# Two layers on one core: attention's query and key projection by seven products, sums shared with the FFN

## The chip, the core and the metric

The kernel runs on one core of a Trainium2 chip, in float32 apart from a few small bf16 operands. Its engines work side by side, each through a queue of its own: TensorE (PE, matmuls), VectorE (DVE), ScalarE (ACT), GpSimd (POOL), and SyncE (SP), which here only starts DMAs. The metric is the device time of one launch in microseconds (us), the median over several runs.

## The reference

Two blocks, each `x = x + mixer(norm(x)) + ffn(norm(x))`, on x of shape (2, 1024, 512): two sequences of 1024 rows.

```python
xn = _layernorm(x, axis=-1)                       # layer 0: a small scan and an FFN
x = x + _L0_attn_ref(xn, ...) + _L0_ffn_ref(xn, ...)
xn = _layernorm(x, axis=-1)                       # layer 1
x = x + _L1_attn_ref(xn, ...) + _L1_ffn_ref(xn, ...)

def _L1_attn_ref(x, W_qkv, b_qkv, W_out, b_out):  # 16 heads of 32
    qkv = x @ W_qkv.T + b_qkv
    q, k, v = jnp.split(qkv, 3, axis=-1)
    scores = jnp.einsum('bqhe,bkhe->bhqk', q, k) * scale
    scores = jnp.where(causal[None, None], scores, -jnp.inf)
    out = jnp.einsum('bhqk,bkhe->bqhe', softmax(scores), v)
    return out.reshape(b, l, d) @ W_out.T + b_out

def _L1_ffn_ref(x, w_gate, w_up, w_down):
    h = silu(x @ w_gate) * (x @ w_up)
    return _sparsify_2to4(h) @ w_down
```

Attention and FFN of layer 1 read the same normalized x, and their outputs are added to the same residual. The change touches the two products that give q and k.

## The kernel before

**Stages.** Layer 0 comes first. Then comes layer 1's attention, with the last rows of layer 0's result normalized and transposed in its opening. Layer 1's FFN comes last. The normalized input of layer 1 is held transposed in four tiles `xt1[0..3]`, each 128 partitions x 4 x 512: the four are chunks of 128 of the 512 input features, the 512 are rows of x. `xt1[0]` and `xt1[1]` belong to the first sequence, `xt1[2]` and `xt1[3]` to the second.

**Seven products.** A product of two matrices cut into 2 x 2 blocks takes eight block products. Strassen's scheme in Winograd's form takes seven, with sums of blocks formed beforehand (t1 to t4 on the side of x, s1 to s4 on the side of the weights) and with the seven results added into the four blocks of the output. Layer 1's FFN is already computed this way: `combine_x` (L148) forms the sums of x on DVE (L156, L157, L160, L161; t1, t2 and t4 in tiles of their own, t3 over the first half of the second x), `combine_w` (L165) those of the weights on POOL, and `gate_up` (L186) issues the seven products (L179). The projection of q and k is computed with all eight.

**Attention.** The work is cut into eight units u: a sequence times a group of four heads (`units`, L1020; four groups, `HG`). Between two units lies what is called a boundary below. For each unit and for each of its tiles of 128 queries, `maxima` (L1079) computes the scores once only for their row maxima: the matmuls "m" (L1088, 4 heads of 32 rows each, the two pairs of heads in two PSUM pairs), the causal mask on the diagonal block (DVE, L1095) and the reduction (DVE, L1096). `larger` (L1106) joins the maxima of two column halves. `shift_part` and `shift_rows` (L1116 to L1130) turn the maxima into three bf16 rows. `weights` (L1136) computes the scores again, transposed (the matmuls "s", L1145), adds the shift (L1151), applies exp (ACT, L1162) into `pt` (or `acc` for the first key tile), and cuts the diagonal block to its triangle (POOL, L1171). `gather` (L1180) multiplies with the values (the matmuls "o", L1191) and adds `pt` into `acc` on POOL (L1198). `total` and `divide` sum `acc` over the partitions, take the reciprocal on DVE and multiply `att` by it on POOL (L1222).

**The order of work.** There are 96 slots n, 12 for each unit, after 13 slots of prologue (n from -13 to -1; the loop L1365). In a slot PE does: s of slot n, o of slot n-1, m of slot n+13 (so the maxima run a good unit ahead), and then one "part": two matmuls of 128x512 of the other products of this layer, so q and k (`project`, "pq"), the values (`values`, "pv"), or the output projection (`project_out`, "po"). `piece` (L1024) cuts each of those into two parts, which fill one PSUM bank over four steps of k; the result is taken from the bank after the second part, for q and k by ACT with the bias (L1052). The parts wait in the list `rest` with a first and a last slot each; `one_part` (L1332) takes the one with the earliest last slot, and `late` (L1352) takes more than one in a slot where the last slots ask for it. Other steps are fixed to a slot with `put`, and follow its part. `in_program_order` (L48) binds PE, DVE, ACT and POOL from the mark L1364 on to the order in which this Python code issues instructions; SP's DMAs follow their own. Each of these engines works through its queue in that order, and an instruction that waits holds up all behind it.

**PSUM.** Three pairs of banks (`ps_wide`) rotate among m (two at a time), s (two), and the small transposes; each must be read empty before it is used again. Of the two single banks, bank 0 holds o and bank 1 serves the parts; while there is no o, in the prologue and at the end, parts alternate between the two (`alone`).

**Before and after attention.** Unit 0's q and k are computed in one run of 16 matmuls before the prologue (L1360); the weights of a head group (`wqk`) are loaded by SP. After the last slot the FFN's first input sums are asked for (L1389) and the rest of the output projection follows. The FFN's units are (`pb`, `g`, `half`) (L1405): `pb` is the sequence, `g` a quarter of the hidden width. Its second sequence's sums are asked for by a second `combine_x` inside the FFN.

## Time and profile before

| | us |
|---|---|
| median of 3 runs (1817.91 to 1819.95) | 1819.89 |
| the profiled execution | 1816.24 |
| span of its trace | 1814.5 |
| end of layer 0, first matmul of unit 0's q and k | 665.97 |
| first m (unit 0) | 681.51 |
| first s (unit 0) | 733.52 |
| first product of layer 1's FFN | 1222.77 |

The granted TensorE clock was 0.999. The rows shown below are of four kinds. In the page's first part each engine has its busy time and its number of instructions. In a table of windows each row is a stretch of the span, with its length and with the busy time of PE, PEld (weight load), DVE, ACT and POOL, then the granted clock, the DMA share and their rate. In a timeline each row is a run of like instructions: start, length, engine, line of the kernel, operation, output and inputs by the program's names, shape, and count; in square brackets stands a wait that ended just before and what ended it. A 128x512 float32 matmul has two records. Times of a row are microseconds from the start of the span; lines such as L1088 are those of the kernel above.

### The profile page before, as it was taken

The page shows a single profiled execution, that of the slowest core. Times are in us where ns is not written, and L with a number is a line of the kernel's source. Part 1 is how long each engine was busy: PE and PEld are TensorE (multiplying, and loading weights), DVE is VectorE, ACT ScalarE, POOL GpSimd, SP SyncE. Part 2 cuts the span into 40 slices and gives each one's busy share as a digit, 9 for nine tenths or more (in the row PEclk, how much of TensorE's full clock was granted, in tenths as well). Part 3 has the DMA queues.
Part 4 walks back from the last instruction along what each step waited for, and adds up shares of the span by engine and source line. Part 5 has one row for each costly group of instructions (what it writes and reads, how often), then busy time and mean ns, then how long its engine had stood idle before and what let it go on. Part 6 is the DMA issues. An engine that isn't in the chain of part 4 may idle for free.

```text
span 1814.5 us, 18967 instructions
## 1 busy us (share of the span) xinstructions
PE 1784.9 (98%) x7386; PEld 915.2 (50%) x7386; DVE 1140.8 (63%) x1483; ACT 476.5 (26%) x681; POOL 806.5 (44%) x697
## 2 busy tenths in 40 slices
PE   9999999999999999999999999999999999999999
PEld 5456566555555564333333333334465555555545
DVE  4875544556544448566677666762868778768675
ACT  3322222122221102334333443422212211212220
POOL 5144554355642222467668756613243344243400
PEclk9999999999999999999999999999999999999999
DMA  6120111111101000000001000011010102201101
GB/s 233 47 81 24 47 35 35 28 43 35 35 23 35 12 29 24 1 12 13 13 1 36 12 13 1 25 47 44 26 58 27 55 24 73 89 25 47 47 1 47
DMA packets 29609, 68.12 MB, mean 38 GB/s; under 512 B 3408, under 2 KB 11856, under 8 KB 27984
## 3 DMA queue, kind: packets, MB, share of 16 engines
q1 hardware_dynamic: 28800, 66.61, 11.3%
q8 instruction: 59, 0.97, 0.2%
q10 hardware_dynamic: 720, 0.30, 0.1%
q14 instruction: 30, 0.25, 0.0%
HBM read 62.70 MB, written 4.19 MB: 37 GB/s over the span
## 4 chain that ended last, share of the span: by engine, by line
PE 92%; DVE 5%; ACT 1%; issue 1%; POOL 0%; POOLq 0%; DVEq 0%; ACTq 0%
PE p_a L179 21%; PE p_c L179 20%; PE d L305 19%; PE pq L1036 6%; PE m L1088 5%; PE s L1145 4%; PE o L1191 3%; PE pv L1036 3%; PE po L1036 3%; PE dr L1526 2%; ACT acc L1162 1%; PE s L1151 1%; PE w L1210 1%; PE pp L603 1%; PE pw L439 1%
## 5 line engine op out<-in xcount | busy, mean ns | idle before, releaser
L323 POOL TENSOR_TENSOR x<-x,de 128x512 f32<-128x512 f32 x87 | 126.5, 1469 | 302.1 <-DVE x L318 168.0
L1198 POOL TENSOR_TENSOR acc<-acc,pt 128x1024 f32<-128x1024 f32 (+3 forms) x138 | 233.8, 1717 | 0.0
L1096 DVE TENSOR_REDUCE tops<-m 128x2 f32<-128x1024 f32 (+2 forms) x192 | 180.9, 956 | 58.8 <-PE m L1088 54.3
L318 DVE TENSOR_TENSOR x<-x,d 128x512 f32<-128x512 f32 x145 | 99.3, 685 | 145.5 <-PE d L305 145.3
L1162 ACT ACTIVATE pt<-s 128x1024 f32<-128x1024 f32 (+3 forms) x160 | 115.2, 766 | 177.4 <-PE s L1151 162.2
L305 PE MATMUL d<-td,h 128*128 128x256 f32 x592 | 141.4, 383 | 4.9 <-DVE h L280 4.9
L305 PEld LDWEIGHTS d<-td,h 128*128 128x128 f32 x592 | 113.2, 192 | 48.0 <-issue 29.2
L1036 PE MATMUL pq<-xt,wqk 128*128 128x512 f32 x256 | 124.2, 614 | 0.0
L179 PE MATMUL p_c<-xt,s_c 128*128 128x512 f32 x256 | 115.2, 593 | 3.4 <-DVE e_c L232 3.4
L179 PE MATMUL p_a<-xt,s_a 128*128 128x512 f32 x256 | 116.8, 599 | 0.9 <-DVE e_a L232 0.9
L179 PE MATMUL p_a<-xt,w 128*128 128x512 f32 x256 | 115.4, 593 | 0.7 <-ACT xt L136 0.7
L179 PE MATMUL p_c<-xt,gu 128*128 128x512 f32 x256 | 115.7, 592 | 0.0
L179 PE MATMUL p_a<-t_a,s_a 128*128 128x512 f32 x256 | 115.3, 594 | 0.0
L179 PE MATMUL p_c<-t_c,s_c 128*128 128x512 f32 x256 | 114.6, 592 | 0.0
L1095 DVE TENSOR_TENSOR m<-m,mask 128x256 f32<-128x256 f32 x128 | 54.7, 427 | 84.6 <-PE m L1088 82.5
L1088 PE MATMUL m<-qk,qk 32*128 32x512 f32 (+3 forms) x768 | 102.8, 533 | 3.9 <-ACT acc L1162 3.0
L1145 PE MATMUL s<-qk,qk 32*128 32x512 f32 (+3 forms) x768 | 93.8, 533 | 0.2 <-DVE tops L1096 0.2
L172 POOL TENSOR_TENSOR s_c<-gu,s_c 128x512 f32<-128x512 f32 x16 | 20.4, 1274 | 136.6 <-PE p_c L179 136.6
L179 PEld LDWEIGHTS p_a<-xt,s_a 128*128 128x128 f32 x256 | 47.5, 191 | 59.0 <-issue 58.4
L1088 PEld LDWEIGHTS m<-qk,qk 32*128 32x128 f32 x768 | 39.8, 183 | 72.7 <-issue 24.8
L179 PEld LDWEIGHTS p_c<-xt,s_c 128*128 128x128 f32 x256 | 48.5, 190 | 55.5 <-issue 54.3
L1036 PEld LDWEIGHTS pq<-xt,wqk 128*128 128x128 f32 x256 | 44.3, 189 | 62.5 <-issue 59.5
(250 smaller groups left out, 3049.7 us busy)
## 6 DMA issues: line engine op xcount, KB each, us to landing
w<-in_W SPq DMA_DIRECT2D x32, 512.0 KB, 3.6
gu<-in_gu SPq DMA_DIRECT2D x32, 512.0 KB, 3.6
wd<-in_down SPq DMA_DIRECT2D x8, 1024.0 KB, 4.8
x<-in_x SPq DMA_DIRECT2D x16, 256.0 KB, 4.6
w2h<-in_W2q SPq DMA_DIRECT2D x4, 1024.0 KB, 11.4
xr<-in_x SPq DMA_DIRECT2D x16, 256.0 KB, 2.7
wqk<-in_WqkvT SPq DMA_DIRECT2D x16, 256.0 KB, 3.2
out_x<-x SPq DMA_DIRECT2D x15, 256.0 KB, 2.0
```

The lines of the kernel that those rows point to most:

```text
L179: nc.tensor.matmul(pair[:, m, :], a[:, m, k, :], x[:, k, :], start=start and k == 0, stop=stop and k == 1, skip_group_check=True,)
L305: nc.tensor.matmul(out_[:, j, :], lhs[:, q, j * P : (j + 1) * P], rhs[:, q], start=m in (0, 1, 3, 4) and j == q == 0, stop=j == q == 1, sk ...
L318: nc.vector.tensor_add(r, r, out_)
L323: nc.gpsimd.tensor_add(r, r, u2[half])
L1036: nc.tensor.matmul(got[0], lhs(k), rhs(k), start=(k == 0), stop=(k == KC - 1))
L1088: nc.tensor.matmul(pair[h // 2][:, h % 2, :e], q[rows, qt * P : (qt + 1) * P], k[rows, c * 512 : c * 512 + e], start=True, stop=True,)
L1095: nc.vector.tensor_add(d, d, mask.unsqueeze(1).to_broadcast([P, 2, P]))
L1096: nc.vector.tensor_reduce(out=tops[u][:, c, qt, 2 * p : 2 * p + 2], in_=pair[p][:, :, :e], axis=mybir.AxisListType.X, op=ALU.max,)
L1145: nc.tensor.matmul(pair[h // 2][:, h % 2, s:], k[rows, kt * P : (kt + 1) * P], q[rows, cols], start=True, stop=False,)
L1162: nc.scalar.activation(pt[:, :, s:], pair[p][:, :, s:], AF.Exp, scale=1.0 / math.sqrt(HD))
L1191: nc.tensor.matmul(po[rows, s:], v[:, rows], pts[h // 2][:, h % 2, s:], start=(kt == 0), stop=last, tile_position=(0, h * HD),)
L1198: eng.tensor_add(acc[:, :, s:], acc[:, :, s:], pt[:, :, s:])
```

## The change

The projection of a unit's q and k becomes one chain of seven products. The weights of q and k of a head group are seen as blocks: w11, w12 (q, first and second half of the input features) and w21, w22 (k). The other side is x and y, the two 512-row halves of the unit's sequence, each in its two halves of features. So output blocks are q of x's rows, q of y's rows, and the same for k.

- `project(u)` yields seven parts of two matmuls (n from 0 to 6) in place of eight. Part 0 fills a bank of its own (chain "b"), parts 1 to 4 run on in one bank (chain "a"), whose contents are read after each of them, and parts 5 and 6 share a third (chain "c"). Results go to q and k by ACT (`first`, with the bias) or are added to them by DVE (`more`). In units 1 to 7 ACT takes the bank after parts 0, 2, 3 and 4, and DVE after 1, 5 and 6; since part 2 goes on adding into the bank that part 1 left, it waits for that DVE addition. Unit 0 takes the parts in the order 1, 0, 2, 5, 3, 6, 4, with bank 0 for chain "a" and bank 1 for "b" and "c"; there DVE takes them after 0, 3 and 6.
- The sums of weights go to POOL: three when a unit's first part is issued (`weight_sums`), and a fourth after part 0. Each is 128x256. One is formed in place in w21, the last in w12.
- The sums of x (`input_sums`): for the first sequence five DVE operations in the run before the prologue, ahead of unit 0's products; for the second five POOL operations, put after the parts of slots 24, 25, 28 and 29. t1, t2 and t4 stay in the tiles that `combine_x` uses. t3 is kept in two tiles of the pool of `att`, since the values need y as it is.
- `own_place`, on POOL in slot 52, forms the FFN's t3 over the first half of y of the second sequence, once the values have been taken from it.
- The FFN takes the second sequence first (`for pb in (1, 0)`), because the tiles t1, t2 and t4 hold its sums then. The `combine_x` at the end of attention goes, and the one within the FFN now forms the first sequence's.
- In `rest` a unit has one entry with seven parts instead of four with two. Its last slot is as before. Its first slot is as before, but for the first unit of the second sequence (u = 4) three later. All other parts, fixed steps and loads are asked for in the slots that they had.

```diff
@@ -145,11 +145,15 @@
-    def combine_x(pool, x, y, name):
-        tt = [
+    def three_sums(pool, name):
+        return [
             pool.tile([P, 2, TT], F32, tag=f"t{n}", name=f"t{n}_{name}") for n in (1, 2, 4)
         ]
+    def combine_x(pool, x, y, name):
+        tt = three_sums(pool, name)
         tt.insert(2, y[:, :2, :])
         def first():
@@ -940,6 +944,7 @@
     first_gu = {}
     sums = ctx.enter_context(tc.tile_pool(name="sums", bufs=1))
     with tc.tile_pool(name="b", bufs=1, reuse_waits="tile") as b:
@@ -1021,17 +1026,21 @@
         alone = 0
+        def next_bank(name):
+            nonlocal alone
+            if alone is not None:
+                alone += 1
+            return ps_bank(name, 1 if alone is None else alone % 2)
         def piece(name, lhs, rhs, done):
             got = []
             def part(n):
                 if n == 0:
-                    nonlocal alone
-                    if alone is not None:
-                        alone += 1
-                    got.append(ps_bank(name, 1 if alone is None else alone % 2))
+                    got.append(next_bank(name))
                 for k in (2 * n, 2 * n + 1):
                     nc.tensor.matmul(
                         got[0], lhs(k), rhs(k), start=(k == 0), stop=(k == KC - 1)
@@ -1041,23 +1050,89 @@
             return [(part, 0), (part, 1)]
-        def project(u, m, n):
+        tts = {}
+        def input_sums(bb):
+            x, y = xt1[2 * bb], xt1[2 * bb + 1]
+            t1, t2, t4 = three_sums(sums, f"b{bb}")
+            t3 = [b.tile([P, TT], F32, tag="att", name=f"t3{k}_{bb}", bufs=12) for k in range(2)]
+            tts[bb] = [t1, t2, t3, t4]
+            e = nc.gpsimd if bb else nc.vector
+            yield e.tensor_sub(t1, y[:, :2, :], x[:, :2, :])
+            yield e.tensor_sub(t2, y[:, 2:, :], t1)
+            yield [e.tensor_sub(t3[k], y[:, 2 + k, :], y[:, k, :]) for k in range(2)]
+            yield e.tensor_sub(t4, x[:, 2:, :], t2)
+        def own_place():
+            y = xt1[3]
+            nc.gpsimd.tensor_sub(y[:, :2, :], y[:, 2:, :], y[:, :2, :])
+            tts[1][2] = y[:, :2, :]
+        def project(u):
             bb, hg = units[u]
-            def done(pq):
-                if (u, m) not in qk:
-                    qk[u, m] = b.tile([P, S], F32, tag=f"qk{m}", name=f"qk{m}_{u}", bufs=3)
+            got = {}
+            order = (1, 0, 2, 5, 3, 6, 4) if u == 0 else range(7)
+            def place(m, n):
+                return qk[u, m][:, n * TT : (n + 1) * TT]
+            def first(m, n, bank):
                 nc.scalar.activation(
-                    qk[u, m][:, n * TT : (n + 1) * TT], pq, AF.Identity,
-                    bias=bqk[:, m * HG + hg : m * HG + hg + 1],
-                )
-            return piece(
-                f"pq_{u}_{m}_{n}", lambda k: wqk[hg][:, k, m, :],
-                lambda k: xt1[2 * bb + n][:, k, :], done,
-            )
+                    place(m, n), bank, AF.Identity, bias=bqk[:, m * HG + hg : m * HG + hg + 1]
+                )
+            def more(m, n, bank):
+                nc.vector.tensor_add(place(m, n), place(m, n), bank)
+            def weight_sums(w11, w21, w22):
+                got[2], got[3] = (
+                    sums.tile([P, 2, P], F32, tag=f"sq{n}", name=f"sq{n}_{u}") for n in (2, 3)
+                )
+                nc.gpsimd.tensor_sub(got[3], w11, w21)
+                nc.gpsimd.tensor_add(w21, w21, w22)
+                nc.gpsimd.tensor_sub(got[2], w21, w11)
+            def part(n):
+                x, y = xt1[2 * bb], xt1[2 * bb + 1]
+                t1, t2, t3, t4 = tts[bb]
+                w11, w12, w21, w22 = (
+                    wqk[hg][:, 2 * e : 2 * e + 2, m, :] for m in range(2) for e in range(2)
+                )
+                if n == order[0]:
+                    if (u, 0) not in qk:
+                        for m in range(2):
+                            qk[u, m] = b.tile([P, S], F32, tag=f"qk{m}", name=f"qk{m}_{u}", bufs=3)
+                    weight_sums(w11, w21, w22)
+                chain = "bbaaaacc"[n + 1]
+                lhs = (w12, w11, got[2], got[3], w22, w21, w12)[n]
+                rhs = (x[:, 2:, :], x[:, :2, :], t2, t3, t4, t1, y[:, 2:, :])[n]
+                start, stop = n in (0, 1, 5), n in (0, 4, 6)
+                if start:
+                    got[chain] = (ps_bank(f"pq_{u}_{chain}", int(chain != "a")) if u == 0 else
+                                  next_bank(f"pq_{u}_{chain}"))
+                for k in range(2):
+                    nc.tensor.matmul(
+                        got[chain], lhs[:, k, :], rhs[k] if type(rhs) is list else rhs[:, k, :],
+                        start=start and k == 0, stop=stop and k == 1, skip_group_check=True,
+                    )
+                do, *at = (
+                    (more, 0, 0), (more, 0, 0), (first, 0, 1), (more, 1, 1), (first, 1, 0),
+                    (more, 1, 1), (more, 0, 1),
+                )[n]
+                if n == order[0] or n == 3 and not got.get("c") or n == 5 and u == 0:
+                    do = first
+                do(*at, got[chain])
+                if n == 0:
+                    nc.gpsimd.tensor_sub(w12, w12, got[2])
+            return [(part, n) for n in order]
         def values(bb, n, j):
@@ -1261,6 +1336,13 @@
             after.setdefault(n, []).append(what)
+        second_sums = []
+        def next_sums():
+            if not second_sums:
+                second_sums.append(input_sums(1))
+            next(second_sums[0])
         sums_at = []
         for u in range(len(units)):
@@ -1274,9 +1356,10 @@
                     put_mid(n + 2 + m, shift_part, u, half, m)
                 put_after(n + 5, shift_rows, u, half)
             if u:
-                lo = per * (u - 2) - 1 if u > 1 else -ahead
-                for x in range(4):
-                    rest.append((lo, per * u - ahead - 1, project(u, x // 2, x % 2)))
+                lo = max(per * (u - 2) - 1, -ahead)
+                if u == HG:
+                    lo += 3
+                rest.append((lo, per * u - ahead - 1, u))
             if u > 1:
                 put(max(per * (u - 2) - 4, -ahead), load_qk, units[u][1])
             for j in range(2):
@@ -1292,6 +1375,10 @@
                     put(len(second) + 1, total, u, j)
         for what in sums_at:
             put_after(*what)
+        rest = [(lo, hi, project(u)) for lo, hi, u in rest]
+        for n in (0, 1, 4, 5):
+            put(per * 2 + n, next_sums)
+        put(per * 4 + 4, own_place)
         for x in range(4):
             rest.append((-ahead, x, values(0, 0, x)))
             rest.append((-ahead, 7 + x, values(0, 1, x)))
@@ -1357,11 +1444,12 @@
                 for last in {x[1] for x in rest}
             )
-        for x in range(4):
-            for f, *args in project(0, x // 2, x % 2):
-                f(*args)
         behind = None
         start = mark()
+        for _ in input_sums(0):
+            pass
+        for f, n in project(0):
+            f(n)
         for n in range(-ahead, len(second)):
             if n == 0:
                 alone = None
@@ -1386,9 +1474,7 @@
         gather(*behind)
         alone = 0
         n = len(second)
-        first_tt, *make = combine_x(sums, xt1[0], xt1[1], "c0")
-        for m, f in enumerate(make):
-            put(n + 5 + m, f)
+        first_tt = tts[1]
         while rest or open_parts or fixed:
             one_part(n)
             what_is_fixed(n)
@@ -1402,7 +1488,7 @@
     start2 = mark()
     with tc.tile_pool(name="c", bufs=1, reuse_waits="tile") as c_:
-        units = [(pb, g, half) for pb in range(2) for g in range(G) for half in range(2)]
+        units = [(pb, g, half) for pb in (1, 0) for g in range(G) for half in range(2)]
         groups = len(units) // 2
         gu_w = dict(first_gu)
@@ -1613,7 +1699,7 @@
                 if at == 5 and n % 2 == 0 and n:
                     load_down(n // 2)
                 if at == 5 and n == len(units) // 2 - 1:
-                    next_tt, first, second = combine_x(sums, xt1[2], xt1[3], "c1")
+                    next_tt, first, second = combine_x(sums, xt1[0], xt1[1], "c1")
                     first()
             gate_up(
```

## The prediction

> **What bounds the kernel now.** First the page's busy times, then the window table, because a mean over five different stages says little about the one that is edited.
>
> ```profile
> PE 1784.9 (98%) x7386; PEld 915.2 (50%) x7386; DVE 1140.8 (63%) x1483; ACT 476.5 (26%) x681; POOL 806.5 (44%) x697
> ```
>
> ```profile
> 666.00:734.00 68.00, 67.88 (x261) 28.95 (x263) 47.92 (x85) 15.70 (x24) 13.20 (x14) 1.00 0.06 16
> 734.00:1158.00 424.00, 416.39 (x2818) 145.83 (x2812) 276.29 (x366) 163.08 (x259) 289.93 (x285) 1.00 0.04 11
> ```
>
> The columns are PE, PEld, DVE, ACT, POOL busy. Attention runs from 666 to 1223. PE is "busy" 98% there, which would make every matmul removed worth its full length. Here the Trainium skill speaks against the change (Perfetto Trace Analysis, Identifying the Most-Contended Engine): matmul busy time is a bad measure, because pipelined matmuls look other than they are. I therefore measure from start to start. A 128x512 fp32 matmul is two records of 429 ns (eight records in 3.43 us in the chain), so 0.858 us. By busy share, 16 fewer matmuls save 13.7 us. By starts, it depends on what a slot costs when its "part" (two 128x512 matmuls, 1.91 us with the change of shape) is not there. One slot of before has none:
>
> ```profile
> 1128.35 1.39 PE L1088 MATMUL m<-qk,qk 32*128 32x512 f32 x8
> ...
> 1130.81 0.70 PE L1145 MATMUL s<-qk,qk 32*128 32x512 f32 x2 [0.16 <-DVE tops L1096]
> ...
> 1133.08 0.76 PE L1088 MATMUL m<-qk,qk 32*128 32x256 f32 x8
> ```
>
> ```profile
> 882.19 1.38 PE L1088 MATMUL m<-qk,qk 32*128 32x512 f32 x8
> 883.50 1.98 PE L1036 MATMUL pq<-xt,wqk 128*128 128x512 f32 x4
> ...
> 887.70 0.94 PE L1088 MATMUL m<-qk,qk 32*128 32x256 f32 x8
> ```
>
> It takes 4.73 us against 5.51 for the same slot with a part. Leaving 1.91 us out saves 0.78: the second half of s waits for the maxima (L1096) to free its PSUM pair, which the part used to cover. Each removed part is therefore costed by its own place. The third view is a boundary between two head groups, PE and POOL, where m of the next group, the last s of the old one and POOL's backlog meet:
>
> ```profile
> 908.92 1.17 PE L1088 MATMUL m<-qk,qk 32*128 32x512 f32 x8
> ...
> 913.59 0.50 PE L1088 MATMUL m<-qk,qk 32*128 32x128 f32 x8
> ...
> 917.30 0.42 PE L1191 MATMUL o<-pt,v 128*32 128x128 f32 x8
> ...
> 922.56 1.07 PE L1191 MATMUL o<-acc,v 128*32 128x512 f32 x8
> ```
>
> ```profile
> 916.36 0.78 POOL L1171 TENSOR_SCALAR_AFFINE_SELECT pt<-pt 128x256 f32<-128x256 f32 x2
> 917.10 2.50 POOL L1198 TENSOR_TENSOR acc<-acc,pt 128x512 f32<-128x512 f32 x2
> 919.54 0.78 POOL L1171 TENSOR_SCALAR_AFFINE_SELECT acc<-acc 128x256 f32<-128x256 f32 x2
> ```
>
> POOL runs without a gap here. Its select of pt ends at 917.14 and o starts 0.16 later: POOL sets this o. Its select of acc ends at 920.32, and the o that reads it starts at 922.56: 2.24 us of slack (1.74 at 797.96/799.70, 2.25 at 1043.64/1045.89).
>
> **The change, part by part** (order of instructions read from the built program; sizes from rows of before).
>
> *Removed:* 8 units x 2 matmuls x 0.858 = 13.7 us of PE, as eight parts. In the new order they are missing at: unit 0's opening run (one); the double part just before the first s (one); an m512 with mask before the 128-wide s (three, at the boundaries of units 0/1, 2/3, 4/5); the m512 before the 256-wide s (two, at 2/3 and 4/5); m128 before s512 in unit 6 (one).
>
> *Unit 0.* Gain 1.72. Products 1 and 0 need no sums and run 665.97 to 669.40. Product 2 needs t2. The old FFN sums of the same tiles give its time:
>
> ```profile
> 666.98 1.22 DVE L156 TENSOR_TENSOR t_c<-xt,xt 128x1024 f32<-128x1024 f32 x1
> 668.23 1.22 DVE L157 TENSOR_TENSOR t_c<-xt,t_c 128x1024 f32<-128x1024 f32 x1
> ```
>
> so t2 is there at 669.45: 0.1 us lost. Product 5 takes the bank that product 0 left, and DVE reads that bank only behind t1, t2, two t3 (0.69 each, as other 128x512 adds) and t4: 669.45 + 1.4 + 1.2 + 0.69 = 672.75, where PE could start at 671.2. Lost 1.6; net 0.0. POOL's three weight sums (0.70 each) follow memsets that end at 664.08, so they should be over at 666.3, before t1 starts. If they start only after the last product of layer 0 (666.2), they meet t1 and t2. The Trainium skill (SBUF — State Buffer, Who interferes with whom) says that a DVE instruction with two SBUF inputs and a GpSimd one that reads SBUF exclude each other. The trace agrees: L1106, 128x16, took 0.17 us with POOL idle and 4.62 at 915.73, ending as POOL stopped. Without the rule the net is 0.0, with it and a late start 1.3 lost. I take 0.0, the memset row being the nearer one, and keep 1.3 for the range.
>
> *Unit 1* (prologue, DVE 47.92 of 68.00 us busy, and 14.03 of 15 between 695 and 710). Gain 1.72. Product 2 follows product 1 directly into the same bank, with DVE's add (0.69, like x<-x,po) between: 0.2 drain + 0.69 + 0.1 = 1.0 lost. The waits for ACT around products 3 and 4 cost about 0.2. Two further adds on the full DVE delay the copies and reductions behind them; followed instruction by instruction, a transpose waits for its pair at 701.1 instead of 699.1, about 0.7 more. Net 0.2 lost (from 1.0 gained, if DVE catches up, to 1.5 lost).
>
> *Steady units.* Parts lie a slot (about 5 us) apart, so three DVE adds of 0.69 and four ACT copies a unit are hidden: the add ends 4.3 to 5.2 us after its m, the next part starts later than 5.6. Without that distance each costs the 1.0 of unit 1. ACT keeps four copies.
>
> *The empty slots.* Masked m512 to the next m128 takes 4.67 us at every boundary (908.92 to 913.59): two mask adds and two 1.22 us reductions, which end just before, with PE's own work some 3.9. Leaving the part out gains nothing there (three times 0.0). The two m512 before a 256-wide s gain 4.54 to 3.83, 0.7 each, but PE then waits for POOL's select of pt (917.14), so nothing is left. The m128 slot of unit 6: s could start at 1126.07, and without the part when ACT frees its pair at 1124.7: gain 1.35. POOL was idle before that unit's second half, so it stays.
>
> *Weight sums on POOL.* Four 128x256 operations a unit; L1198 at 128x256 is 0.70 from start to start, so 2.8 us. For units 2, 4 and 6 they fall where POOL idles and hide. For 3, 5 and 7 they stand in POOL's queue just ahead of the select of acc, in the backlog. Behind them wait that select and then o. With the 0.17 from select to o seen above, o comes at 797.96 + 2.85 + 0.17 = 801.0 (was 799.70), 923.3 (922.56) and 1046.7 (1045.89): lost 1.3, 0.8, 0.8. The fourth also waits for product 0, long over.
>
> *Second sequence's sums on POOL* (t1, t2, t4 2.35 each by L1198 128x1024, t3 two of 1.27). t1 to t3 fit into idle time. t4 stands behind the multiplication of att:
>
> ```profile
> 886.65 1.27 POOL L1222 TENSOR_TENSOR att<-att,inv 128x512 f32<-128x512 f32 x1 [2.89 <-DVE inv L1220]
> ```
>
> so it ends at 890.25, and product 4 of unit 4 is due at 888.57: 1.8 lost. The acc adds behind it start 2.35 later; the idle 2.46 before 899.64 covers that. own_place (2.35) falls into a like idle stretch and is hidden; without it, product 3 of unit 6 would wait up to 2 us.
>
> *FFN.* Same instructions in the same order on other tiles; one DVE subtraction (1.16, L160) goes, off the path. The loads and SP's queue keep their order. 0.0.
>
> *Sum:* 0.0 - 0.2 - (1.3 + 0.8 + 0.8) - 1.8 + 1.35 = 3.55 us longer. The profiled span is 1814.5 (execution 1816.24); it becomes 1818.0. The median of the runs shown, 1819.89, lies 3.65 over its own profiled execution; on it the sum gives 1823.4.
>
> **Rivals.**
> *PE-bound after all, faster.* POOL's queue gives way at the boundaries, because it is served sooner than I read it. Then units 0 and 1 keep 1.7 each, the two 256-wide slots 0.7 each and unit 6 1.35: 6.2 shorter, 1813.7. For it: POOL has 134 us idle between 734 and 1158. Against it: the 0.16 at 917.30. It decides if the three selects of acc end less than 1.7 to 2.2 us later than now.
> *DVE locked out by POOL, slower.* L1106 already took 4.6 us at three boundaries, until POOL paused. If POOL's run is 2.8 longer without a pause, the next reductions and the second half of s come 2.5 to 3 later in three places instead of 0.8 to 1.3, and unit 0 meets its 1.3: about 6 more, 1829.5. Against it: each weight sum waits for the one before, which should leave a pause.
> *Nothing moves.* t4 and the prologue are absorbed by slack that I have not seen: 0 to 2 longer, 1821.
>
> **How the numbers follow.** Forecast 0.50 (alone 1821 to 1826.5), lock-out 0.25, faster 0.17, nothing 0.08. A measurement of this kernel can tell about 0.2%, 3.6 us, and the forecast lies on that line: 0.27 of its 0.50 above. Slower 0.27 + 0.25 = 0.52; same 0.23 + 0.08 = 0.31; faster 0.17. The range takes the forecast, nothing and nearly all of lock-out: 1815 to 1831.
>
> **What would show it.** pq at 7/8 of its matmuls; PE waiting on DVE twice before the first m of unit 1; o of acc 0.8 to 1.3 late with POOL's new sums before it; about 1.8 us of PE waiting on POOL for t4; FFN span unchanged. I am wrong if o of acc doesn't wait on POOL, or if stage times outside attention move by over 1 us.

## The result, and the profile after

The changed kernel takes 1826.61 us (median of 5 runs, 1824.40 to 1828.52), the kernel before 1819.10 (5 runs, 1816.78 to 1819.95) beside it: ratio 1.0044, 95% interval 1.0029 to 1.0058. It is slower by 7.5 us, and the interval lies wholly above 1. The forecast was 3.55 slower, 1823.4, with a range of 1815 to 1831. The profiled execution of the changed kernel is 1825.55, its span 1823.8, which is 9.3 over the span before.

The page's first part and two rows of its window table, in the same columns as before:

```profile
PE 1780.7 (98%) x7354; PEld 913.7 (50%) x7354; DVE 1147.9 (63%) x1508; ACT 476.8 (26%) x681; POOL 841.3 (46%) x735
```

```profile
666.00:734.00 68.00, 63.82 (x245) 27.30 (x243) 51.26 (x86) 15.70 (x24) 21.20 (x22) 1.00 0.08 25
734.00:1158.00 424.00, 406.25 (x2757) 143.11 (x2756) 275.14 (x384) 162.09 (x256) 309.88 (x308) 0.99 0.04 11
```

PE has 32 records less (7386 to 7354; 16 matmuls are gone), POOL 35 us more. The clock column of the second row reads 0.99 where it read 1.00. That hundredth is three stretches of 3.41 us at half clock (3 x 0.5 x 3.41 / 424 = 0.012), and much of what follows is about them.

To find the places, I compared the start of every o (one for each slot) in the two traces, counted each from its span's start, and noted where the difference grows:

| stretch | forecast | measured |
|---|---|---|
| layer 0, up to unit 0's first product (665.97, 667.62) | 0 | +1.65 |
| unit 0, to the first m | 0.0 (1.3 if POOL collides with DVE) | +1.21 |
| unit 1 and prologue, to the first o (739.55, 743.14) | +0.2 | +0.73 |
| boundary of units 0/1 | +1.3 | +1.58 |
| boundary 1/2 | 0 | +0.50 |
| t4, slot 30 | +1.8 | +1.73 |
| boundary 2/3 | +0.8 | +1.02 |
| boundary 3/4 | 0 | -0.56 |
| boundary 4/5 | +0.8 | +0.90 |
| slots 61 to 72 | 0 | -0.07 |
| unit 6, slot 76 | -1.35 | -1.07 |
| FFN | 0 | +1.71 |
| sum | +3.55 | +9.33 |

Boundary 2/3 of the changed kernel, PE and POOL (the stretch that was shown of before):

```profile
915.77 1.14 PE L1163 MATMUL m<-qk,qk 32*128 32x512 f32 x8
...
918.84 0.38 PE L1220 MATMUL s<-qk,qk 32*128 32x128 f32 x2 [1.63 <-DVE tops L1171]
...
919.98 0.98 PE L1266 MATMUL o<-pt,v 128*32 128x256 f32 x8 [0.59 <-POOL pt L1246]
920.89 0.50 PE L1163 MATMUL m<-qk,qk 32*128 32x128 f32 x8
921.32 3.68 PE L1121 MATMUL pq_b<-xt,wqk 128*128 128x512 f32 x4
...
930.96 1.06 PE L1266 MATMUL o<-acc,v 128*32 128x512 f32 x8
```

```profile
924.49 2.50 POOL L1273 TENSOR_TENSOR acc<-acc,pt 128x512 f32<-128x512 f32 x2
926.94 0.74 POOL L1097 TENSOR_TENSOR sq<-wqk 128x256 f32<-128x256 f32 x1
...
930.04 0.77 POOL L1246 TENSOR_SCALAR_AFFINE_SELECT acc<-acc 128x256 f32<-128x256 f32 x2
```

From m512 to m128 the slot takes 5.12 us here (4.67 before; the 0.59 of waiting for POOL's select of pt is in it) and 4.67 at the boundary 0/1. So the empty slot gives nothing, as forecast. But the product behind it, the same four records as ever, takes 3.68 us instead of 1.98. The weight sums are where they were expected, and the select of acc ends at 930.81; o of acc starts at 930.96 and shows no wait for it.

The window table again, for the stretches around the three masked empty slots; the column to read is the clock, third from the right (1.00 or 0.50):

```profile
791.76:795.17 3.41, 1.86 (x24) 0.98 (x24) 2.86 (x4) 0.38 (x1) 3.41 (x5) 1.00 0.00 0
795.17:798.58 3.41, 3.41 (x12) 1.17 (x4) 2.15 (x5) 0.38 (x1) 3.41 (x5) 0.50 0.00 0
918.05:921.47 3.42, 2.04 (x25) 1.10 (x26) 2.25 (x4) 0.38 (x1) 3.42 (x5) 1.00 0.00 0
921.47:924.88 3.41, 3.41 (x4) 0.92 (x4) 3.02 (x5) 0.38 (x1) 3.41 (x5) 0.50 0.00 0
1040.93:1044.35 3.42, 1.20 (x17) 0.64 (x16) 3.08 (x4) 0.38 (x1) 3.42 (x5) 1.00 0.01 2
1044.35:1047.76 3.41, 3.41 (x17) 1.60 (x12) 1.81 (x5) 0.38 (x1) 3.41 (x3) 0.50 0.02 5
```

Each time PE is busy for 1.2 to 2.0 of 3.41 us, and the next 3.41 us run at half clock. The distances between these stretches are whole multiples of that length: 921.47 - 795.17 = 126.30 = 37 x 3.413, 1044.35 - 921.47 = 122.88 = 36 x 3.413. The Trainium skill (TensorE: Matmul & The Clock Gate, Part 1: The HAM clock gate) describes this: a monitor looks at PE's activity in windows of 3413 ns that run free of the kernel, and halves the clock after an idle one. The length and the spacing agree with the trace. "Idle" does not: windows with 35% to 60% of PE busy were enough here.

Two rows of the table of stretches (layer 0 and the FFN) are not the change's. Layer 0 of this execution has 6.83 us at half clock from 23.76, the one before had 3.41 from 151.71; the programs don't differ there. In the FFN both kernels have the same stall, before and after:

```profile
1295.81 3.67 PE L179 MATMUL p_c<-xt,s_c 128*128 128x512 f32 x8 [2.48 <-DVE e_c L232]
```

```profile
1303.44 5.37 PE L183 MATMUL p_c<-xt,s_c 128*128 128x512 f32 x8 [2.49 <-DVE e_c L236]
```

A stall of 2.48 us was followed by full clock, one of 2.49 by 3.41 us at half (1303.76). Where the windows fall differs from execution to execution, and with it one such event, 1.7 us. Without these two rows the change costs 9.33 - 1.65 - 1.71 = 5.97 us in this trace.

A half-clock window of 3.41 us takes 0.5 x 3.41 / 1815 = 0.00094 off the mean granted clock. The runs before lie mostly at 0.997 and 0.998, the five runs after at 0.993 to 0.995: some 2 to 5 such windows more, each worth up to 1.7 us. An estimate of their share: of later runs of the kernel before, the six at 0.994 and 0.995 took 1821.4 to 1822.4, and the changed kernel took 1824.4 to 1828.5 at the same two clocks. So of the 7.5 us some 3 go with the clock, and some 4 do not.

### The profile page after: what moved, and what is told of

Same layout as the page of the kernel before. It is cut to its first block, busy times and chain, and to the rows that moved or that the text cites. A ratio compares the mean times of both kernels' runs of the same rounds, so it can differ in the third digit from the quotient of the medians.

```text
span 1823.8 us, 18993 instructions
## 1 busy us (share of the span) xinstructions
PE 1780.7 (98%) x7354; PEld 913.7 (50%) x7354; DVE 1147.9 (63%) x1508; ACT 476.8 (26%) x681; POOL 841.3 (46%) x735
## 4 chain that ended last, share of the span: by engine, by line
PE 89%; DVE 6%; POOL 2%; ACT 2%; issue 1%; DVEq 0%; ACTq 0%; POOLq 0%
PE p_a L183 21%; PE p_c L183 20%; PE d L309 19%; PE m L1163 4%; PE s L1220 4%; PE pv L1045 3%; PE o L1266 3%; PE po L1045 3%; PE pq_a L1121 3%; PE dr L1612 2%; PE pq_c L1121 1%; POOL acc L1273 1%; DVE tops L1171 1%; ACT acc L1237 1%; PE pp L607 1%
## 5 line engine op out<-in xcount | busy, mean ns | idle before, releaser
L1220 PEld LDWEIGHTS s<-qk,qk 32*128 32x128 f32 x768 | 34.3, 183 | 81.8 <-issue 69.8
L183 PEld LDWEIGHTS p_c<-xt,gu 128*128 128x128 f32 x256 | 48.6, 190 | 51.0 <-issue 49.5
L183 PEld LDWEIGHTS p_a<-t_a,s_a 128*128 128x128 f32 x256 | 48.4, 194 | 50.4 <-issue 49.8
```

The source lines that it names most:

```text
L183: nc.tensor.matmul(pair[:, m, :], a[:, m, k, :], x[:, k, :], start=start and k == 0, stop=stop and k == 1, skip_group_check=True,)
L1220: nc.tensor.matmul(pair[h // 2][:, h % 2, s:], k[rows, kt * P : (kt + 1) * P], q[rows, cols], start=True, stop=False,)
```

## The experiments

Two theories for the boundaries. **POOL** is the forecast's: the weight sums delay the select of acc, and o with it. **Clock**: the empty slot leaves a window with little matmul work, and the half clock behind it costs 1.6. A third has both, running beside each other, so that taking one away shows nothing. Times of the kernel before in these comparisons are medians of 24 to 42 runs, 1817.2 to 1817.8, so 1.3 to 1.9 lower than the 1819.10 that stood beside the changed kernel. The changed kernel was not timed again; where a run is compared with it, the distance of each to its own run of before is the fairer measure (7.5 us for the changed kernel). Readings by boundary come from one profiled execution of each kernel.

### Filling the slots, moving the sums, and both

Filled:

```diff
             if n >= 0 or n % 2:
-                one_part(n)
+                if not one_part(n) and n in (10, 34, 58):
+                    spare = ps_bank(f"spare_{n}", 1)
+                    for k in range(2):
+                        nc.tensor.matmul(
+                            spare, xt1[0][:, k, :P], xt1[1][:, k, :], start=k == 0, stop=k == 1
+                        )
```

> The changed kernel, with two 128x512 matmuls whose result nobody reads put into the three slots that the change left empty at the boundaries 0/1, 2/3 and 4/5 (slots 10, 34, 58). Base: the changed kernel, 1826.6 us. In its trace PE idles 1.63 to 1.72 us in these slots, the granted clock is 0.5 for the next 3.41 us, and the first q/k product takes 3.59 us instead of 1.98; o of acc starts 0.15 to 0.23 us after POOL's select of acc ends. Theory two limits at once (the halved clock costs 1.6 at each boundary, and POOL's queue, longer by the weight sums, ends at the same time): no halved clock at the boundaries, but o of acc then waits for POOL; 0 to 0.8 shorter, about 1826.2. Clock alone: 3 x 1.6 = 4.8 shorter, 1821.8. POOL alone (the prediction's step): no change, 1826.6.

Sums later (the four sums in one function, the two tiles taken where they were):

```diff
...
-                    weight_sums(w11, w21, w22)
+                    new_sums()
+                    if u in (3, 5, 7):
+                        put(per * (u - 2), all_sums, w11, w12, w21, w22)
+                    else:
+                        three(w11, w21, w22)
...
-                if n == 0:
+                if n == 0 and u not in (3, 5, 7):
```

> The changed kernel, with the four weight sums of units 3, 5 and 7 put into POOL's queue one slot later, behind the select of acc. Base 1826.6 us. Two limits at once: PE still runs at half clock there, so o of acc starts as late as before; within 0.5, 1826.6. Clock alone: the same, 1826.6. POOL alone: o of acc comes 1.3, 0.8 and 0.8 earlier, 2.9 shorter, 1823.7.

Both edits together:

> Both edits: the three empty slots filled with matmuls that nobody reads, and the weight sums of units 3, 5 and 7 one slot later. Base 1826.6 us. Two limits at once: each boundary gets its 1.6 back only now, 4.8 shorter, 1821.8 (o of acc again starts 1.7 us or more after the select, as before the change). Clock alone: 1821.8 too, but the first of the three runs had it already. POOL alone: 2.9 shorter, 1823.7, as the second run.

Medians: filled 1827.47 (ratio to before 1.0044, 1.0027 to 1.0061), later 1827.19 (1.0053, 1.0038 to 1.0068), both 1826.27 (1.0040, 1.0018 to 1.0062). They lie 9.9, 9.6 and 8.7 over before. The first two are near what the theory of two limits says, but the medians alone decide nothing: the third missed its 1821.8 by far, and half clock at other places, told below, is in all three. So the traces have to say more. What the boundaries cost against before, from the starts of o:

| boundary | changed | filled | later | both |
|---|---|---|---|---|
| 0/1 (slots 11 to 13) | +1.58 | +1.37 | +1.63 | +0.30 |
| 2/3 (slots 35 to 37) | +1.02 | +0.89 | -0.19 | -0.19 |
| 4/5 (slots 59 to 61) | +0.90 | +0.89 | +1.02 | +0.26 |

With the slots filled no window at the boundaries is at half clock, and o of acc now waits for POOL at each of them (1.06, 1.17 and 1.18 us), which no trace had shown so far. At the first:

```profile
801.66 0.72 POOL L1133 TENSOR_TENSOR wqk<-wqk,sq 128x256 f32<-128x256 f32 x1
802.34 0.77 POOL L1246 TENSOR_SCALAR_AFFINE_SELECT acc<-acc 128x256 f32<-128x256 f32 x2
```

```profile
802.80 1.41 PE L1266 MATMUL o<-acc,v 128*32 128x512 f32 x8 [1.06 <-POOL acc L1246]
```

With the sums moved the half clock stays at 0/1 and 4/5, and the time with it; at 2/3 no half clock came in that execution, and the loss is gone. With both edits each boundary gets most or all of its time back. So both limits are real, they run beside each other, and each alone costs about what the other does.

What ate the gain of "both" is the clock at other places. Its profiled execution has half clock for 13.65 us from 1131.77 and for 3.41 from 739.24; slots 76 to 78 come out 4.7 us later than in before, where the changed kernel gained 1.07. The run with filled slots has the same 13.65 us there (from 1131.57, 4.7 later), the run with later sums 6.83 (from 1131.70, 1.8 later); so it is in part chance that their medians come so near to the changed kernel's. Slots 76 and 77 are two empty slots in a row: the changed kernel left the first, the second was empty already. The clock stays down there for four windows although PE is busy throughout by the trace; that the stretch, at half clock, holds too little work in a window to get the clock back is a likely reason, not a shown one. The same slots cost nothing in the profiled execution of the changed kernel. The five runs of "both" lie between 1819.56 (clock 0.999) and 1831.89 (0.991). At like clock the gain is there: "both" took 1819.56 at 0.999 and 1823.30 at 0.997, so about 1821.4 between them, where the one filled run at 0.998 took 1823.91. The columns of the table differ by 2.8 in sum. These are single runs.

### Fewer matmuls in the kernel before

This run asks the question directly: the kernel before, and only work taken away.

```diff
+                half = name in ("pv_0_1_3", "pv_1_0_3", "pq_6_1_1")
-                for k in (2 * n, 2 * n + 1):
+                for k in () if half and n else (2 * n, 2 * n + 1):
...
-                        got[0], lhs(k), rhs(k), start=(k == 0), stop=(k == KC - 1)
+                        got[0], lhs(k), rhs(k), start=(k == 0), stop=(k == (1 if half else KC - 1))
```

> The kernel before, with six 128x512 matmuls left out and nothing else changed: the second halves of one value product each in slots 10 and 34 and of one key product in slot 58 (two steps of k of four, so these three 128x512 results are computed over half of the features only). What follows them on DVE and ACT stays. Base: the kernel before, 1817.2 us. Clock theory: without these parts PE idles 1.6 to 1.7 us at the three boundaries, the next 3.41 us run at half clock, and each boundary comes out 1.6 later; less 0.5 at 2/3 and 4/5, where the lock-out of the join of maxima is then covered: 3.5 to 4.0 longer, 1821. Work theory (PE is the bound, less work is less time): 6 x 0.43 to 6 x 0.86 = 2.6 to 5.2 shorter, 1812 to 1814.6. Neither (empty slots hidden behind DVE, clock unchanged): 1817.2.

1822.08 us (22 runs) against 1817.77 (30): ratio 1.0021, 1.0014 to 1.0028. Six matmuls fewer make the kernel 4 us slower. The mean clock accounts for it: its median over the runs is 0.994 against 0.997, and at equal clock the two kernels take the same (at 0.994, 1822.0 to 1822.5 with six fewer and 1822.1 to 1822.2 before; at 0.996, 1818.9 to 1820.2 and 1819.4 to 1820.8). The three boundaries of its profiled execution are a test by themselves, since the same edit meets the windows in three ways:

```profile
786.09:789.50 3.41, 1.82 (x20) 0.73 (x12) 2.00 (x4) 0.95 (x2) 3.41 (x3) 1.00 0.00 0
789.50:792.91 3.41, 3.21 (x27) 1.66 (x28) 3.20 (x6) 0.77 (x2) 3.41 (x5) 1.00 0.00 0
908.97:912.38 3.41, 1.69 (x21) 1.01 (x20) 2.18 (x4) 0.41 (x1) 3.41 (x3) 1.00 0.00 0
912.38:915.79 3.41, 3.40 (x22) 1.53 (x19) 2.65 (x5) 0.77 (x2) 3.41 (x4) 0.50 0.00 0
915.79:919.21 3.42, 3.42 (x8) 1.05 (x10) 0.94 (x3) 0.00 (x0) 3.42 (x5) 0.50 0.02 5
```

```profile
789.63 0.38 PE L1146 MATMUL s<-qk,qk 32*128 32x128 f32 x2 [1.72 <-DVE tops L1097]
911.97 0.38 PE L1146 MATMUL s<-qk,qk 32*128 32x128 f32 x2 [1.72 <-DVE tops L1097]
```

PE waits 1.72 us for DVE in slot 10 and in slot 34 alike. At 0/1 no half clock follows, and o starts 0.00 later than in before: the empty slot is free, and worth nothing. At 2/3 two windows run at half clock and o of slot 35 is 2.77 late; at 4/5 one (from 1038.67), and o of slot 59 is 1.62 late. There are no weight sums in this kernel. So the half clock alone makes such a loss.

The same rows show what stays open. PE was busy for 1.82 of 3.41 us in the window that nothing followed and for 1.69 in the one that was followed by half clock, but for 1.86 and 2.04 in two of the changed kernel that were followed too. Busy time doesn't separate them. At the boundaries the low windows hold mostly the narrow matmuls of m, s and o (32 rows or 32 columns), and few of 128x512. An estimate that counts this separates better: give each float32 record 0.43 us for every 512 columns that it streams, and weigh it by the share of 128 rows and 128 columns that it uses. In the twelve traces, between 655 and 1760 us, all 29 full-clock windows that were followed by half clock come out under 0.40 of a window; of the 3817 others eight lie under 0.36. What the monitor counts was not measured.

### t4, and DVE's order in unit 0

```diff
-        for n in (0, 1, 4, 5):
+        for n in (0, 1, 3, 4):
...
-        for _ in input_sums(0):
-            pass
-        for f, n in project(0):
-            f(n)
+        make, run = input_sums(0), project(0)
+        for step in (make, make, run, run, make, make, run, run, run, run, run):
+            if step is make:
+                next(make)
+            else:
+                f, n = run.pop(0)
+                f(n)
```

> The changed kernel with two small moves, far apart in time. (a) t3 and t4 of the second sequence one slot earlier (slots 27 and 28 in place of 28 and 29), so that t4 stands ahead of the multiplication of att in POOL's queue. Prediction's step: product 4 of unit 4 no longer waits (1.66 us of idle PE at 894), 1.7 shorter. Rival: POOL is the limit of the whole stretch, and the wait returns at a later product, 0. (b) In unit 0, DVE's addition of product 0 ahead of t3 and t4, not behind. Prediction's step: product 5 finds its bank free, the wait of 1.43 us at 674 goes, 1.4 shorter. Rival: DVE is then late with t3 or t4 for products 3 and 4, 0 to 0.5 shorter. Both: 1826.6 - 3.1 = 1823.5 us.

1822.61 us (18 runs; 1.0029, 1.0022 to 1.0036), 4.0 below the changed kernel's median, or 2.5 by the distances to before (5.1 against 7.5), where 3.1 was expected. In the changed kernel t4 stood behind the multiplication of att, and product 4 waited for it:

```profile
892.33 1.28 POOL L1297 TENSOR_TENSOR att<-att,inv 128x512 f32<-128x512 f32 x1 [2.89 <-DVE inv L1295]
893.56 2.35 POOL L1065 TENSOR_TENSOR t_b<-xt,t_b 128x1024 f32<-128x1024 f32 x1
```

```profile
895.97 1.98 PE L1121 MATMUL pq_a<-t_b,wqk 128*128 128x512 f32 x4 [1.66 <-POOL t_b L1065]
```

With t4 one slot earlier, slot 30 adds 0.00 instead of 1.73. In unit 0 product 5's wait of 1.43 us is gone, and the unit takes 15.06 us from its first product to the first m instead of 16.75 (15.54 before). That is a gain of 0.48, where matmuls worth 1.72 have gone. Most of the rest is POOL's collision with DVE, seen in both kernels (product 2 waits 0.96 us for POOL in the changed one and 0.97 in this); of the changed one, POOL and DVE:

```profile
667.92 0.73 POOL L1097 TENSOR_TENSOR sq<-wqk 128x256 f32<-128x256 f32 x1 [2.20 <-issue]
668.74 1.72 POOL L1098 TENSOR_TENSOR wqk<-wqk 128x256 f32<-128x256 f32 x1
670.54 1.59 POOL L1099 TENSOR_TENSOR sq<-wqk 128x256 f32<-128x256 f32 x1
```

```profile
669.91 1.63 DVE L1063 TENSOR_TENSOR t_b<-xt,t_b 128x1024 f32<-128x1024 f32 x1
671.46 2.34 DVE L1064 TENSOR_TENSOR t<-xt 128x512 f32<-128x512 f32 x2
```

The sums began not with the end of the memsets but 0.30 after the first product's start, 0.14 after the last matmul of layer 0 ends; the profile names nothing that held them ("issue"). Then POOL's 0.73 becomes 1.72 and 1.59, DVE's 1.22 becomes 1.63 and two of 0.69 become 2.34.

### The join of maxima as a reduction, in the kernel before

The forecast had leaned on L1106 as evidence for the exclusion of DVE and POOL, and named as a rival that longer POOL runs would lengthen it. The edit gives it one input in SBUF instead of two:

```diff
-            nc.vector.tensor_tensor(top[:, 0], top[:, 0], top[:, 1], ALU.max)
+            bigger[u] = sm.tile([P, NJ, 4], F32, tag="bigger", name=f"bigger_{u}", bufs=2)
+            nc.vector.tensor_reduce(
+                out=bigger[u], in_=top.rearrange("p c q h -> p q h c"),
+                axis=mybir.AxisListType.X, op=ALU.max,
+            )
...
-            top = left[u, half][:, m - 1] if m else tops[u][:, 0, qs]
+            top = left[u, half][:, m - 1] if m else bigger[u] if half else tops[u][:, 0, qs]
```

> The kernel before, with only the join of maxima changed: a reduction over one SBUF input in place of a maximum of two. Base: the kernel before, 1817.6 us. Lock-out theory (a DVE instruction with two SBUF inputs waits while POOL works from SBUF): the three joins of 4.6 us take 0.2 to 0.3, and s and o behind them come 0.5 earlier at the boundaries 2/3, 3/4 and 4/5: 1.5 shorter, 1816.1. Rival (any small DVE instruction beside POOL is held): still 4.6, no change, 1817.6.

The groups of this line, of before and of the edited kernel (eight instructions; busy time, then the mean in ns):

```profile
L1106 DVE TENSOR_TENSOR tops<-tops 128x16 f32<-128x16 f32 x8 | 17.3, 2162 | 0.0
```

```profile
L1107 DVE TENSOR_REDUCE bigger<-tops 128x16 f32<-128x32 f32 x8 | 1.4, 178 | 0.0
```

Each takes 0.18 to 0.19 us beside the same POOL work where three had taken 4.6. The Trainium skill's rule (SBUF — State Buffer, Who interferes with whom) has this side too: a DVE instruction with at most one SBUF input, outside the modes that use two ports, does not contend. The boundaries 2/3, 3/4 and 4/5 come 0.52, 0.52 and 0.59 earlier, 1.6 in sum, of which 1.2 is left at the last o. In the time it doesn't show: 1816.91 (13 runs) against 1817.24 (42), ratio 1.0001, 0.9993 to 1.0009. That side of the expectation is unproven. In the changed kernel this exclusion fits the rows with no forecast: at 1/2 the join took 3.69 us (0.72 before, o +0.50), at 3/4 it took 0.51 (4.61 before, o -0.56). In two other traces a join of 3.69 at another boundary brought the same: o +0.60 at slot 72 of "both" and of the run with empty slots elsewhere.

### Empty slots elsewhere, and everything together

```diff
-            if n >= 0 or n % 2:
+            if (n >= 0 or n % 2) and n not in (5, 25, 29, 49, 53, 73):
                 one_part(n)
```

> The changed kernel, with the empty slots moved and nothing else: parts may not start in slots 5, 25, 29, 49, 53 and 73, so that slots 10, 33, 34, 57, 58 and 76 have one again. Base: the changed kernel, 1826.6 us. Theory clock: what the three boundaries lost was a half-clock window of 3.41 us each, brought on by a stretch with little matmul work; in the new places the neighbours keep PE at work, so none of the three is left (-4.8), o of acc then waits for POOL as in the run with filled slots (+1.4, +1.1, +1.0), t4 has two slots more (-1.7), and six empty slots in places that PE limits give 0.8 to 1.1 each (-5.5, less 1.1 that slot 76 gave): 8 to 9 shorter, about 1818. Rival POOL alone (empty slots cost nothing, the weight sums do): only t4's 1.7 and up to 2 from the new places, 1823 to 1825.

1821.84 us (19 runs; 1.0022, 1.0015 to 1.0029), 4.6 over before against 7.5: 2.9 shorter than the changed kernel by these distances, where 8 to 9 were expected. By the time alone this is also what "POOL alone" allows (1.6 to 3.6 shorter); the trace decides. In it no boundary is at half clock, and o of acc waits for POOL as in the run with filled slots (+1.4, +0.9, +0.9). Slots 5, 29 and 53 give 0.79 each at their own o and 0.18 more at the next, 0.97 as expected, but 25, 49 and 73 only 0.25 to 0.28. Two half-clock windows are new (from 738.32 and 1168.40, some 1.5 each), and slot 31 loses 0.54. So the sizes of the three weak slots were one error, and the clock at new places the other.

Then this, with the edits shown so far and one for unit 1:

```diff
-            order = (1, 0, 2, 5, 3, 6, 4) if u == 0 else range(7)
+            order = (1, 0, 2, 5, 3, 6, 4) if u < 2 else range(7)
...
-                    got[chain] = (ps_bank(f"pq_{u}_{chain}", int(chain != "a")) if u == 0 else
+                    got[chain] = (ps_bank(f"pq_{u}_{chain}", int((chain != "a") == (u == 0))) if u < 2 else
...
-                if n == order[0] or n == 3 and not got.get("c") or n == 5 and u == 0:
+                if n == order[0] or n == 3 and not got.get("c") or n == 5 and u < 2:
```

> Everything that the traces ask for at once: empty slots spread as in the run before, weight sums of units 3, 5 and 7 one slot later, t3 and t4 one slot earlier, unit 0 with DVE's addition of product 0 ahead of t3 and t4, unit 1 in unit 0's order of products on fixed banks, and the join of maxima as a reduction over one input instead of a maximum of two. Base: the kernel before, 1817.6 us in the last comparison. By the terms measured so far: boundaries 0.3 longer each at most, t4 0, unit 0 and the prologue 0.5 shorter to 0.5 longer, six empty slots 0.8 to 1.1 each shorter, three lock-outs of 0.5 gone: 5 to 7 shorter, 1811 to 1813. If the half clock comes back at other places (two low windows in a row), 1.7 is lost for each: 1815 and more.

1817.68 us (13 runs; 1.0001, 0.9992 to 1.0009), which misses its 1811 to 1813. The same without the line for the empty slots:

> As the run with everything, but the empty slots left where the change put them (10, 33, 34, 57, 58, 76). Base: the changed kernel, 1826.6 us. Clock theory: t4 1.7, unit 0 and 1 together 1.4 to 2.3 and the joins 0.5 shorter, but the boundaries stay at half clock and the weight sums are hidden behind it: 1822 to 1823, some 10 longer than with the empty slots spread. If the place of the empty slots doesn't matter: within 2 of the run with everything.

1822.41 us (6 runs; 1.0029, 1.0018 to 1.0041), with two boundaries at half clock in its trace (from 912.78 and 1039.08). Where the six empty slots lie is worth 4.7 us.

The trace of the version with everything names one edit that hurt: unit 1 in unit 0's order of products loses 1.40 from the first m to the first o, twice the 0.73 of the changed kernel. The second version leaves that edit out, and puts all empty slots where one had given 0.79, into the sixth slot of a unit:

```diff
-            if (n >= 0 or n % 2) and n not in (5, 25, 29, 49, 53, 73):
+            if (n >= 0 or n % 2) and n not in (5, 17, 29, 41, 53, 65):
```

> Second version of all edits: empty slots in 5, 17, 29, 41, 53 and 65 (each the sixth slot of a unit), weight sums of units 3, 5 and 7 one slot later, t3 and t4 one slot earlier, unit 0 with DVE's addition of product 0 ahead of t3 and t4, the join of maxima as a reduction; unit 1 as the change has it. Base: the kernel before, 1817.2 us; the first version with everything was 1817.7. By terms of that run: the three empty slots that gave 0.28 give 0.79 here (1.5 shorter), the prologue loses 0.7 instead of 1.4: 2.2 shorter than the first version, 1815.5, if no half-clock window comes in addition. If the spare time of the sixth slot is taken back by POOL at the next boundary, 1817.5.

1813.73 us (9 runs, 1813.10 to 1815.25) against 1817.77 (30): ratio 0.9975, 0.9965 to 0.9984. This version beats both kernels, by 4 us the one before and so by some 12 the change as it was made. In its trace the six slots give 0.97 each (0.79 at their own o, 0.18 at the next), 5.8 in sum, the joins 1.6, unit 0 0.5; the sums moved behind the select still cost 0.3 at three boundaries, and the prologue 0.7. Two half-clock windows remain in the last unit (6.83 us from 1158.96, where no parts are left to issue; 1.7 lost) and one behind the FFN's stall (1.7).

## Why the prediction was right, and where it was not

- **The sign and the range** held: slower, 1826.61 in 1815 to 1831, but by twice the forecast's 3.55. That an empty masked slot gains nothing, because it waits for DVE, held to the hundredth: it took 4.67 us from m to m at 0/1, and in the kernel with six matmuls fewer it moved o by 0.00 where the clock stayed full. The slots before those at 2/3 and 4/5 gained 0.55 and lost it again in the next, as worked out.
- **The boundaries** (forecast 2.9, measured 3.5) are the step that failed. The sizes were near by luck: the cause is not the one that sets o in the trace of the changed kernel. POOL's delay exists: 1.4, 0.9 and 0.9 appear when the slots are filled. In the change as made it is covered by a loss of 1.5 to 1.6 that the working did not have, the half clock behind an empty slot; with the sums out of the way, 1.6 and 1.0 remain at 0/1 and 4/5. "Leaving the part out gains nothing there (three times 0.0)" should have read: gains nothing, and may cost 1.6 or more. The forecast's own signs of being wrong were both met in this trace: o of acc shows no wait for POOL, and layer 0 and the FFN moved by 1.65 and 1.71. The first points at this step; the second turned out to be half-clock windows that the change does not bring.
- **t4**: forecast 1.8, measured 1.73, for the reason given. Shown by moving it.
- **Unit 0**: the row that I took (sums over at 666.3, net 0.0) was wrong, the other branch (1.3 lost) right, at 1.21: the sums start after the end of layer 0's matmuls.
- **Unit 1**: the two waits are there at the sizes worked out (0.94 at 687.73 for the addition, 0.71 at 704.07 for the transposes). The net was 0.73 and not 0.2, within the stated 1.0 gained to 1.5 lost.
- **Unit 6**: 1.07 gained for 1.35. But these two adjacent empty slots can also cost 4.7, as two runs had it.
- **Rival of the lock-out**: its part in unit 0 came true, at the boundaries it went the other way. That its 1829.5 lies no farther from the result than the forecast's 1823.4 says nothing for it. The late PE moved the joins away from POOL's long runs at three boundaries and into one at another, 1.1 gained in sum (0.5 each at 2/3, 3/4 and 4/5, less 0.5 at 1/2).
- **FFN** 0.0: the order of the sequences costs nothing that can be seen; the 1.71 is one half-clock window behind a stall that before has too. The run with filled slots has the changed kernel's FFN without that window, and loses 0.02 there; the kernel before with only its join changed has the window, from 1296.07.

The term that was missing in the sum is thus the clock, beside a POOL delay that is real but covered. In the trace of before its granted clock was 0.999, and I took that for a constant.

## What to carry to other kernels

Matmuls that hide behind another engine's work are not only worthless to remove, they can be what keeps TensorE's clock up. Before taking them out, ask which 3.4 us then hold little matmul work, and put the gap where PE itself sets the pace and its neighbours are full. When two edits each change nothing, try them together before you drop either: two limits may end at the same time.

## What was not expected of the hardware

- Half clock followed stretches of 3.41 us in which PE was still busy 35% to 60% of the time at the boundaries, and up to 78% elsewhere in attention (2.66 of 3.41 us from 1128.16 with filled slots). It came in whole multiples of 3.41 us (6.83 and 13.65 too).
- In a stretch of mostly narrow matmuls the clock stayed down for four such windows (1131.6 to 1145.2), with PE busy throughout by the trace.
- The same stall of 2.48 or 2.49 us is followed by half clock in one execution and not in another. Most of the scatter between runs of one kernel goes with their mean clock: the kernel with six matmuls fewer took 1817.4 at 0.997, 1820.0 to 1820.6 at 0.995 and 1824.5 to 1825.2 at 0.992.
